# A new order of issue for a four-layer graph-attention kernel: the planner's durations read from a trace, and a weight-load term in every handoff to TensorE

## The chip, the cores and the metric

The kernel runs on one core of one Trainium2 chip. The metric is the time of one execution on the device in microseconds (us); less is better. The time of a version is the median of its runs.

## What is computed

The input `x` is 128 graphs of 64 nodes with 512 features in 32-bit floats, 8192 rows in all; `adj` is one 64x64 adjacency that all graphs share. Four layers follow one another, each of the same outer form:

```python
h = jnp.maximum(_layernorm(x, axis=-1), 0.0)
x = x + layer(h, adj, ...)
```

Layers 0 and 1 are attention with 8 heads of 64 features inside each graph, masked by `adj` (q, k, v projections of 512x512, softmax over 64 neighbours, weighted sum; layer 1 has an output projection too). Layer 2 has no softmax:

```python
rel = jnp.einsum('bnd,bmd->bnm', q, k)
rel = adjacency.T[None, :, :] * rel
rel = rel / jnp.linalg.norm(rel, axis=2, keepdims=True)
return jnp.einsum('bnm,bmd->bnd', rel, v)
```

Layer 3 is masked attention like layer 1 with an output projection `o`, and returns `o + layernorm(o)`.

## The kernel before

The rows are cut into 16 pieces of 512 rows (8 graphs each); 16 pieces by 4 layers make 64 turns of the main loop, `n` from 0 to 63. The activations pass from layer to layer through DRAM. In each turn a piece is normalised, transposed by a 16-bit DMA transposition (`turn`: a copy to `z` on VectorE or ScalarE, the transposition `hp<-z` on SyncE's queue, a copy back to `hT` or `s` on ScalarE), and projected. A projection is a fast matrix product: seven products of halves instead of eight, and three of the seven are cut once more (`prod_2`). For that GpSimd and VectorE form sums of inputs (`S` and `S2` from `hT`, `SO` and `SO2` from `oT`) and of weights, and ScalarE, VectorE and GpSimd recombine the products that lie in PSUM into `qT`, `kT`, `v`, `xo` and small helpers `p5`. A step that takes products out of a PSUM bank is called an eviction here (`kT<-mm`, `v<-mm` and so on). Scores (`mm<-kT,qT`) and weighted values (`mm<-s,v` or `mm<-v,s`) are blocks of small 64x64 products; `attend` between them is the softmax on all four engines.

No line of the kernel issues an instruction directly. `pe`, `dve`, `act`, `gps` and `plan.sync` are recorders: each call becomes a step of a `Plan` (`record`, `add`), with what it must wait for, a duration and a delay to its users, both from `duration`. A run of matmuls between `plan.begin()` and `plan.end()` is one step, a block. `Plan.order` then puts all 13,182 steps in an order: it walks through time, and takes for the engine that can start first the ready step that can start first, and among steps that can start equally early the one with the lowest `rank`. The rank is the latest time a step may have for the matmuls that need it, plus `PREFER`, a table with an offset in ns for some kinds of step, less `HASTE` for a step of another engine that reads PSUM. The same walk gives each block its PSUM bank out of eight; `WINDOW` limits how many banks out of turn may be opened. `issue` then issues in that order. Each engine runs its own instructions strictly in the order of issue and waits on semaphores where data or banks need it. So the table and the durations are guesses at build time: they decide the order and the banks, and nothing else. All instructions carry the line of `issue`, L285, in the profile, so groups are told apart by tiles.

The two numbers that a step leaves for its users are used like this:

```python
ready[u] = max(ready[u], at + busy - lag + (0.0 if same and not moves else late))
last[h] = max(last.get(h, 0.0), at + busy + (0.0 if e == "tensor" else late))
```

The first is the time at which the user `u` is taken to be ready, the second the time at which a PSUM bank is taken to be free again.

Of the kernel before, what the change touches and what calls it, by code (L numbers as in the profile page):

```python
# [21 lines left out]
D = 512  # L22
# [34 lines left out]
class Plan:  # L57
# [106 lines left out]
    def order(self):  # L164
# [58 lines left out]
        while len(self.start) < n:  # L223
# [40 lines left out]
            for h in uses[i]:  # L264
                last[h] = max(last.get(h, 0.0), at + busy + (0.0 if e == "tensor" else late))
                left[h] -= 1
                if not left[h]:
                    del holds[self.bank[h]]
                    freed[self.bank[h]] = last[h]
            for u, lag in users[i]:  # L270
                same = self.steps[u][0] == e
                ready[u] = max(ready[u], at + busy - lag + (0.0 if same and not moves else late))
                wait[u] -= 1
                if not wait[u]:
                    here[self.steps[u][0]].append(u)
# [35 lines left out]
class Pool:  # L311
# [28 lines left out]
PORT = 150.5  # L340
# [6 lines left out]
WINDOW = 6  # L347
RESERVE = 0
HASTE = 0.0
PREFER = {  # L350
    "gps dma_start out_0_dram<-xo 2048": -12683,
    "gps dma_start x1<-kT": -7145,
    "gps dma_start x1<-row": -3460,
    "gps dma_start x1<-xo": -18648,
    "gps memset mhalf<- 8": 4917,
    "gps memset ones<- 1": -3867,
    "gps tensor_scalar ve<-mv 1": 622,
    "gps tensor_scalar ve<-mv 4": -1287,
    "gps tensor_tensor S2<-S 128": 9247,
    "gps tensor_tensor S2<-S2 128": -37406,  # L360
    "gps tensor_tensor S<-S 512": -89087,
    "gps tensor_tensor S<-hT 512": -1496,
    "gps tensor_tensor SO2<-SO 128": 12636,
    "gps tensor_tensor SO2<-SO2 128": 10398,
    "gps tensor_tensor SO<-oT 512": 2203,
    "gps tensor_tensor hT<-hT 128": 1226,
    "gps tensor_tensor kT<-kT 128": 5636,
    "gps tensor_tensor kT<-kT 256": 3369,
    "gps tensor_tensor kT<-kT 512": -42897,
    "gps tensor_tensor oT<-oT 128": 2476,  # L370
    "gps tensor_tensor qT<-qT 128": -134,
    "gps tensor_tensor qT<-qT 256": -1241,
    "gps tensor_tensor rn<-ss 8": -17140,
    "gps tensor_tensor row<-hT 128": -1603,
    "gps tensor_tensor row<-row 128": 8443,
    "gps tensor_tensor rs<-ve 1": 12875,
    "gps tensor_tensor s<-hT 128": -26189,
    "gps tensor_tensor s<-s 1024": -13182,
    "gps tensor_tensor s<-s 128": -40765,
    "gps tensor_tensor v<-v 128": -615,  # L380
    "gps tensor_tensor w<-w 128": -892,
    "gps tensor_tensor w<-w 512": 3785,
    "gps tensor_tensor xo<-xo 128": 44131,
    "gps tensor_tensor xo<-xo 512": -445,
    "sca activation kT<-mm 128": -119261,
    "sca activation kT<-mm 256": -39612,
    "sca activation qT<-mm 128": -41982,
    "sca activation qT<-mm 256": -11513,
    "sca activation s<-s 1024": 49040,
    "sca activation s<-s 256": 11077,  # L390
    "sca activation xin<-xin 512": 38622,
    "sca copy hT<-hp 1024": 66109,
    "sca copy hT<-mm 512": 10088,
    "sca copy kT<-mm 128": -16208,
    "sca copy kT<-mm 512": -19133,
    "sca copy oT<-mm 512": -12905,
    "sca copy p5<-mm 128": 237,
    "sca copy qT<-mm 128": 625,
    "sca copy qT<-mm 256": 54924,
    "sca copy qT<-mm 512": 3166,  # L400
    "sca copy s<-hp 1024": 447,
    "sca copy s<-mm 512": 10472,
    "sca copy v<-mm 128": 7235,
    "sca copy v<-mm 256": -3409,
    "sca copy v<-mm 512": -11450,
    "sca copy w<-mm 128": -19703,
    "sca copy w<-mm 256": -8441,
    "sca copy xo<-mm 128": 3488,
    "sca copy xo<-mm 256": -4935,
    "sca copy z<-mm 512": 4852,  # L410
    "sca copy z<-s 1024": 11870,
    "syn dma_start SO<-in_L2_gnn_Wk_dram": -11583,
    "syn dma_start a2d<-z": 2446,
    "syn dma_start adj2<-in_adj_dram": 31047,
    "syn dma_start bk0<-in_L0_gnn_bk_dram": 17099,
    "syn dma_start bk1<-in_L1_gnn_bk_dram": 6479,
    "syn dma_start bq0<-in_L0_gnn_bq_dram": -9211,
    "syn dma_start bq1<-in_L1_gnn_bq_dram": 6149,
    "syn dma_start bv1<-in_L1_gnn_bv_dram": 5734,
    "syn dma_start hp<-z": -502,  # L420
    "syn dma_start oT<-in_L2_gnn_Wq_dram": 4334,
    "syn dma_start oT<-in_L2_gnn_Wv_dram": 17636,
    "syn dma_start out_0_dram<-qT": 14773,
    "syn dma_start out_0_dram<-xo": 16686,
    "syn dma_start row<-in_L0_gnn_bv_dram": -25453,
    "syn dma_start row<-in_L3_gnn_ln_beta_dram": -11958,
    "syn dma_start row<-in_L3_gnn_ln_gamma_dram": -3573,
    "syn dma_start w<-a2d": -3983,
    "syn dma_start w<-in_L0_gnn_Wk_dram": 15922,
    "syn dma_start w<-in_L0_gnn_Wq_dram": 27053,  # L430
    "syn dma_start w<-in_L0_gnn_Wv_dram": -942,
    "syn dma_start w<-in_L1_gnn_Wk_dram": -1089,
    "syn dma_start w<-in_L1_gnn_Wo_dram": 29403,
    "syn dma_start w<-in_L1_gnn_Wq_dram": 6765,
    "syn dma_start w<-in_L3_gnn_w_proj_dram": 1486,
    "syn dma_start w<-in_L3_gnn_w_qkv_dram": 11967,
    "syn dma_start xin<-in_x_dram": -293,
    "syn dma_start xin<-out_0_dram": -4629,
    "syn dma_start xin<-x1": -1001,
    "syn dma_start xo<-x1": 599,  # L440
    "ten matmul mm<-S 128": -809,
    "ten matmul mm<-S 256": 1010,
    "ten matmul mm<-SO 128": 6386,
    "ten matmul mm<-SO 256": -1770,
    "ten matmul mm<-hT 128": 131,
    "ten matmul mm<-hT 256": -309,
    "ten matmul mm<-hT 64": 100821,
    "ten matmul mm<-oT 128": 538,
    "ten matmul mm<-oT 256": -850,
    "ten matmul mm<-oT 512": -47270,  # L450
    "ten matmul mm<-qT 64": -5718,
    "ten matmul mm<-row 128": -1010,
    "ten matmul mm<-s 1": 29205,
    "ten matmul mm<-s 128": 916,
    "ten matmul mm<-s 64": 12446,
    "ten matmul mm<-v 64": 3123,
    "ten matmul mm<-w 128": 589,
    "ten matmul mm<-w 256": 3762,
    "ten transpose mm<- 128": 3312,
    "ten transpose mm<-s 128": 34074,  # L460
    "vec bn_aggr mv<-st 2": 22606,
    "vec bn_stats st<-kT 6": 32606,
    "vec bn_stats st<-w 6": 180,
    "vec bn_stats st<-xin 6": 18172,
    "vec reciprocal sr<-sr 16": -12420,
    "vec scalar_tensor_tensor nb<-mv 1": -6732,
    "vec scalar_tensor_tensor nb<-mv 4": 407,
    "vec scalar_tensor_tensor qT<-z 512": 11775,
    "vec scalar_tensor_tensor xo<-mm 256": -18855,
    "vec scalar_tensor_tensor xo<-z 512": 2344,  # L470
    "vec scalar_tensor_tensor z<-kT 512": -2532,
    "vec scalar_tensor_tensor z<-w 512": -7120,
    "vec tensor_copy hT<-mm 512": -34134,
    "vec tensor_copy ss<-mm 4": -8958,
    "vec tensor_copy z<-oT 1024": -28676,
    "vec tensor_copy z<-xin 1024": -1765,
    "vec tensor_reduce mx<-s 16": -1296,
    "vec tensor_reduce sr<-s 16": -539,
    "vec tensor_scalar mask0<-adj2 64": -460,
    "vec tensor_scalar mask1<-adj2 64": 7823,  # L480
    "vec tensor_scalar mask1<-mask1 64": -2796,
    "vec tensor_scalar mask3<-adj2 64": 3491,
    "vec tensor_tensor S2<-hT 128": -8365,
    "vec tensor_tensor S<-S 512": -9486,
    "vec tensor_tensor S<-hT 512": 846,
    "vec tensor_tensor SO2<-oT 128": 21917,
    "vec tensor_tensor hT<-hT 128": 12751,
    "vec tensor_tensor kT<-mm 128": -2068,
    "vec tensor_tensor kT<-mm 512": -895,
    "vec tensor_tensor oT<-mm 512": 569,  # L490
    "vec tensor_tensor oT<-oT 128": 19236,
    "vec tensor_tensor p5<-mm 128": -44354,
    "vec tensor_tensor qT<-mm 128": 1804,
    "vec tensor_tensor qT<-mm 256": 12827,
    "vec tensor_tensor qT<-mm 512": -35526,
    "vec tensor_tensor qT<-qT 512": 13240,
    "vec tensor_tensor s<-mm 512": 311,
    "vec tensor_tensor v<-mm 128": -36409,
    "vec tensor_tensor v<-mm 256": -7501,
    "vec tensor_tensor v<-mm 512": -84,  # L500
    "vec tensor_tensor w<-mm 128": -22071,
    "vec tensor_tensor w<-mm 256": 2131,
    "vec tensor_tensor w<-mm 512": -831,
    "vec tensor_tensor w<-w 128": -8652,
    "vec tensor_tensor w<-w 512": 30518,
# [9 lines left out]
def duration(eng, op, aps, a, k):  # L515
# [3 lines left out]
    if eng == "tensor":  # L519
        kdim, m = aps[1].partition_size(), aps[1].free_size()  # L520
        if op == "transpose":
            return 109, 200
# [1026 lines left out]
```

## Time and profile before

| what | value |
|---|---|
| runs before (three) | 2804.97, 2805.68, 2806.94 us; median 2805.68 |
| the profiled execution: its own time, its span | 2805.3 us, 2803.5 us |
| TensorE matmul busy | 2758.9 us, 98% of the span, 29,259 records |
| TensorE weight load busy (beside the matmuls) | 2506.2 us, 89% |
| VectorE, ScalarE, GpSimd busy | 2185.6 us (78%), 1691.6 us (60%), 1999.4 us (71%) |
| mean granted TensorE clock | 0.999 |
| DMA engines, mean busy share by slice | 0.4 to 0.7 |

The table's busy times are sums over instructions as the profile draws them. Matmul ends are modelled and overlap, so that busy share is no measure of how tightly the matmuls follow each other; starts are. `PE` is the matmul, `PEld` the load of its weights, `DVE` VectorE, `ACT` ScalarE, `POOL` GpSimd, `SP` SyncE with its DMA queue. A bracket behind a row gives the idle time before it and what ended it.

### The profile page before, as it was taken

The page shows a single profiled execution, that of the slowest core. Times are in us where ns is not written, and L with a number is a line of the kernel's source. Part 1 is how long each engine was busy: PE and PEld are TensorE (multiplying, and loading weights), DVE is VectorE, ACT ScalarE, POOL GpSimd, SP SyncE. Part 2 cuts the span into 40 slices and gives each one's busy share as a digit, 9 for nine tenths or more (in the row PEclk, how much of TensorE's full clock was granted, in tenths as well). Part 3 has the DMA queues.
Part 4 walks back from the last instruction along what each step waited for, and adds up shares of the span by engine and source line. Part 5 has one row for each costly group of instructions (what it writes and reads, how often), then busy time and mean ns, then how long its engine had stood idle before and what let it go on. Part 6 is the DMA issues. An engine that isn't in the chain of part 4 may idle for free. (4 is left out here: it accounts for less than half of the span.)

```text
span 2803.5 us, 72722 instructions
## 1 busy us (share of the span) xinstructions
PE 2758.9 (98%) x29259; PEld 2506.2 (89%) x29259; DVE 2185.6 (78%) x4436; ACT 1691.6 (60%) x2885; POOL 1999.4 (71%) x2381
## 2 busy tenths in 40 slices
PE   9999999999999999999999999999999999999998
PEld 8889888988898999999999898989899899898897
DVE  7877778877877777777777666666788998988998
ACT  5677677777665665666755454445555655565662
POOL 5667767668977767677679855556777887887885
PEclk9999999999999999999999999999999999999999
DMA  5765566666466455464566675656545655655655
GB/s 140 155 144 132 145 145 147 150 135 143 95 116 119 91 117 97 94 133 88 100 150 128 158 180 147 166 135 163 110 76 92 114 99 92 116 97 91 116 86 113
DMA packets 635026, 344.54 MB, mean 123 GB/s; under 512 B 484288, under 2 KB 565952, under 8 KB 634688
## 3 DMA queue, kind: packets, MB, share of 16 engines
q1 hardware_dynamic: 601424, 273.83, 42.8%
q0 software_dynamic: 33264, 66.06, 14.7%
q8 instruction: 230, 3.77, 0.5%
q14 instruction: 108, 0.88, 0.1%
HBM read 120.63 MB, written 102.76 MB: 80 GB/s over the span
## 5 line engine op out<-in xcount | busy, mean ns | idle before, releaser
L285 PE MATMUL mm<-S,w 128*128 128x256 f32 (+1 forms) x4600 | 907.0, 338 | 9.2 <-ACT kT L285 6.2
L285 PEld LDWEIGHTS mm<-S,w 128*128 128x128 f32 x4600 | 732.0, 191 | 74.7 <-ACT kT L285 9.6
L285 PE MATMUL mm<-hT,w 128*128 128x128 f32 (+1 forms) x3392 | 605.2, 310 | 5.9 <-ACT kT L285 2.0
L285 PEld LDWEIGHTS mm<-hT,w 128*128 128x128 f32 x3392 | 520.5, 191 | 51.7 <-ACT p L285 2.7
L285 PE MATMUL mm<-w,S 128*128 128x256 f32 (+1 forms) x2604 | 520.4, 339 | 0.8 <-ACT v L285 0.7
L285 PEld LDWEIGHTS mm<-w,S 128*128 128x128 f32 x2604 | 419.0, 191 | 37.5 <-issue 1.0
L285 DVE TENSOR_TENSOR qT<-mm,qT 128x128 f32<-128x128 f32 (+2 forms) x578 | 264.4, 485 | 173.4 <-PE mm L285 82.6
L285 PE MATMUL mm<-w,hT 128*128 128x128 f32 (+1 forms) x1872 | 343.1, 315 | 6.2 <-DVE v L285 4.4
L285 DVE TENSOR_TENSOR kT<-mm,kT 128x512 f32<-128x512 f32 (+2 forms) x616 | 274.4, 471 | 91.3 <-ACT kT L285 68.1
L285 ACT COPY v<-mm 128x128 f32<-128x128 f32 (+1 forms) x380 | 169.4, 447 | 291.7 <-PE mm L285 262.9
L285 ACT COPY hT<-hp 128x1024 uint16<-128x1024 uint16 x252 | 331.0, 1354 | 17.3 <-DMA hp<-z 15.1
L285 PEld LDWEIGHTS mm<-w,hT 128*128 128x128 f32 x1872 | 287.1, 191 | 31.0 <-issue 3.6
L285 DVE TENSOR_TENSOR v<-mm,v 128x512 f32<-128x512 f32 (+2 forms) x578 | 261.1, 480 | 61.9 <-PE mm L285 25.8
L285 PE MATMUL mm<-w,SO 128*128 128x256 f32 x1302 | 262.0, 336 | 5.2 <-DVE kT L285 5.0
L285 POOL TENSOR_TENSOR s<-s,mx 128x1024 f32<-128x1024 f32 x96 | 186.8, 1947 | 109.4 <-DVE mx L285 87.0
L285 ACT ACTIVATE xin<-xin,nb,rs 128x512 f32<-128x512 f32 x256 | 198.8, 814 | 98.5 <-DVE nb L285 98.5
L285 ACT COPY s<-hp 128x1024 uint16<-128x1024 uint16 x188 | 246.2, 1353 | 0.0
L285 POOL TENSOR_TENSOR qT<-qT,p 128x256 f32<-128x256 f32 (+1 forms) x170 | 110.0, 659 | 185.4 <-DVE qT L285 105.5
L285 PEld LDWEIGHTS mm<-w,SO 128*128 128x128 f32 x1302 | 213.6, 191 | 28.5 <-DVE kT L285 10.4
L285 DVE COPY z<-xin 128x1024 uint16<-128x1024 uint16 x252 | 197.8, 801 | 30.3 <-ACT xin L285 29.6
L285 ACT COPY z<-s 128x1024 uint16<-128x1024 uint16 x188 | 191.6, 1049 | 26.4 <-POOL s L285 26.2
L285 POOL TENSOR_TENSOR v<-v,p 128x256 f32<-128x256 f32 (+1 forms) x170 | 124.3, 742 | 96.4 <-DVE v L285 86.1
(120 smaller groups left out, 4685.9 us busy)
## 6 DMA issues: line engine op xcount, KB each, us to landing
xin<-x SPq DMA_DIRECT2D x128, 256.0 KB, 4.7
xin<-in_x_dram SPq DMA_DIRECT2D x64, 256.0 KB, 3.9
x<-row POOLq DMA_DIRECT2D x16, 1024.0 KB, 16.9
xin<-out_dram SPq DMA_DIRECT2D x64, 256.0 KB, 3.9
out_dram<-row POOLq DMA_DIRECT2D x16, 1024.0 KB, 9.3
x<-xo POOLq DMA_DIRECT2D x15, 1024.0 KB, 12.3
out_dram<-xo POOLq DMA_DIRECT2D x15, 1024.0 KB, 9.3
xo<-in_x_dram SPq DMA_DIRECT2D x32, 256.0 KB, 3.9
```

The costliest lines, as they stand in the source:

```text
L285: getattr(getattr(self.nc, eng), op)(*a, **k)
```

## The change

The steps, their instructions and what each must wait for stay as they are. What is changed is what the planner is told, and so the order of issue and the banks:

- A new constant, `LOAD = 110` ns, is added to the delay of every handoff from another engine to TensorE, and to the time at which another engine frees a PSUM bank.
- The durations and delays in `duration` are new, most by a few per cent. Delays of VectorE go from 150 to 160 ns, of ScalarE from 170 to 180 or 200, of GpSimd from 120 to 130; the `PORT` delay from 150.5 to 160.5.
- `WINDOW` goes from 6 to 7 and `HASTE` from 0 to 1865 ns.
- The whole table `PREFER` (some 160 entries) is new.
- The block in `relate` is planned 580 instead of 300 ns longer than its matmuls.

```diff
-                last[h] = max(last.get(h, 0.0), at + busy + (0.0 if e == "tensor" else late))
+                last[h] = max(last.get(h, 0.0), at + busy + (0.0 if e == "tensor" else late + LOAD))
...
                 same = self.steps[u][0] == e
-                ready[u] = max(ready[u], at + busy - lag + (0.0 if same and not moves else late))
+                load = LOAD if self.steps[u][0] == "tensor" else 0.0
+                ready[u] = max(ready[u], at + busy - lag + (0.0 if same and not moves else late + load))
...
-PORT = 150.5
+PORT = 160.5
+LOAD = 110
...
-WINDOW = 6
+WINDOW = 7
 RESERVE = 0
-HASTE = 0.0
+HASTE = 1865.0
 PREFER = {
...
-    "gps tensor_tensor S<-S 512": -89087,
+    "gps tensor_tensor S<-S 512": -646,
...
-    "sca activation xin<-xin 512": 38622,
+    "sca activation xin<-xin 512": 12304,
...
-    "vec tensor_tensor kT<-mm 512": -895,
+    "vec tensor_tensor kT<-mm 512": -1303,
...
-    fixed = {"scalar_tensor_tensor": 140, "tensor_reduce": 100}.get(op, 85)
+    fixed = {"scalar_tensor_tensor": 125, "tensor_reduce": 100}.get(op, 68)
...
-        return fixed + n * 1.01, PORT if two else 150
+        return fixed + n * 1.04, PORT if two else 160
...
-        return max(240 + 0.49 * n, (1.32 if out.dtype == U16 else 1.4 if own else 0.95) * n), 170
+        if out.dtype == U16:
+            return (947 if out.ap[-1][0] == 1 else 1211), 200
+        if psum:
+            return (55 + 0.836 * n, 180) if op == "copy" else (175 + 0.711 * n, 180)
+        return (717 if isinstance(k.get("scale"), bass.AP) else 105 + 0.834 * n), 180
...
-            return (1030 if ALU.pow in a else 250), 120
-        return 1.82 * n if n > D else 170 + 2.1 * n, 120
+            return (385 + 156.5 * n if ALU.pow in a else 200), 130
+        return 1.82 * n if n > D else 143 + 2.13 * n, 130
...
-        plan.end(300)
+        plan.end(580)
```

More of the change, by code (lines that the diff above doesn't have):

```diff
@@ L346 @@
 ON_DVE = "2"
-WINDOW = 6
+WINDOW = 7
 RESERVE = 0
-HASTE = 0.0
+HASTE = 1865.0
 PREFER = {
[L351 to L360, printed above, removed]
-    "gps tensor_tensor S<-S 512": -89087,
[L362 to L390, printed above, removed]
-    "sca activation xin<-xin 512": 38622,
[L392 to L488, printed above, removed]
-    "vec tensor_tensor kT<-mm 512": -895,
[L490 to L505, printed above, removed]
-    "vec tensor_tensor xo<-mm 128": -8130,
-    "vec tensor_tensor xo<-mm 512": 843,
@@ new lines @@
+    "gps dma_start out_0_dram<-row 2048": -5236,
+    "gps dma_start out_0_dram<-xo 2048": -402,
+    "gps dma_start x1<-kT": -8963,
+    "gps dma_start x1<-row": 1362,
+    "gps dma_start x1<-xo": -9912,
+    "gps tensor_scalar ve<-mv 1": -564,
+    "gps tensor_tensor S2<-S 128": 3948,
+    "gps tensor_tensor S2<-S2 128": -5548,
+    "gps tensor_tensor S<-S 128": 11385,
+    "gps tensor_tensor S<-S 512": -646,
+    "gps tensor_tensor S<-hT 512": 589,
+    "gps tensor_tensor SO2<-SO 128": -17575,
@@ new lines @@
+    "gps tensor_tensor SO2<-SO2 128": -2154,
+    "gps tensor_tensor SO<-SO 128": -411,
+    "gps tensor_tensor SO<-oT 512": -362,
+    "gps tensor_tensor hT<-hT 128": 3311,
+    "gps tensor_tensor kT<-kT 128": -98339,
+    "gps tensor_tensor kT<-kT 512": -2966,
+    "gps tensor_tensor qT<-qT 128": -5579,
+    "gps tensor_tensor qT<-qT 256": 9110,
+    "gps tensor_tensor rn<-ss 8": -34892,
+    "gps tensor_tensor row<-hT 128": 664,
+    "gps tensor_tensor row<-row 128": 928,
+    "gps tensor_tensor rs<-ve 1": 47293,
@@ new lines @@
+    "gps tensor_tensor rs<-ve 4": -1991,
+    "gps tensor_tensor s<-hT 128": 1720,
+    "gps tensor_tensor s<-s 1024": -27587,
+    "gps tensor_tensor s<-s 128": -447,
+    "gps tensor_tensor v<-v 128": -51403,
+    "gps tensor_tensor v<-v 256": 1536,
+    "gps tensor_tensor w<-w 128": -3400,
+    "gps tensor_tensor w<-w 256": -2153,
+    "gps tensor_tensor w<-w 512": -7294,
+    "gps tensor_tensor xo<-xo 128": -3829,
+    "gps tensor_tensor xo<-xo 256": -17821,
+    "gps tensor_tensor xo<-xo 512": -24461,
@@ new lines @@
+    "sca activation kT<-mm 128": 3117,
+    "sca activation kT<-mm 256": -44222,
+    "sca activation qT<-mm 128": -3862,
+    "sca activation qT<-mm 256": 7208,
+    "sca activation s<-s 1024": -9262,
+    "sca activation s<-s 256": 461,
+    "sca activation xin<-xin 512": 12304,
+    "sca copy hT<-hp 1024": 72415,
+    "sca copy hT<-mm 512": -23177,
+    "sca copy kT<-mm 128": 26150,
+    "sca copy kT<-mm 256": -8365,
+    "sca copy kT<-mm 512": 12936,
+    "sca copy oT<-mm 512": 24886,
+    "sca copy qT<-mm 256": -9312,
@@ new lines @@
+    "sca copy qT<-mm 512": 9418,
+    "sca copy s<-hp 1024": -12125,
+    "sca copy v<-mm 128": 1565,
+    "sca copy v<-mm 512": -4871,
+    "sca copy w<-mm 128": 23360,
+    "sca copy w<-mm 256": -22055,
+    "sca copy xo<-mm 128": -291,
+    "sca copy xo<-mm 256": -422,
+    "sca copy xo<-mm 512": -6652,
+    "sca copy z<-hp 1024": 2677,
+    "sca copy z<-mm 512": -2648,
+    "sca copy z<-s 1024": 1031,
+    "syn dma_start SO<-in_L2_gnn_Wk_dram": -5858,
+    "syn dma_start a2d<-z": 238,
+    "syn dma_start adj2<-in_adj_dram": 19924,
@@ new lines @@
+    "syn dma_start bk0<-in_L0_gnn_bk_dram": -7662,
+    "syn dma_start bk1<-in_L1_gnn_bk_dram": 24005,
+    "syn dma_start bq0<-in_L0_gnn_bq_dram": -9601,
+    "syn dma_start bq1<-in_L1_gnn_bq_dram": 2267,
+    "syn dma_start bv1<-in_L1_gnn_bv_dram": -5413,
+    "syn dma_start hp<-z": -14040,
+    "syn dma_start oT<-in_L2_gnn_Wq_dram": -137,
+    "syn dma_start oT<-in_L2_gnn_Wv_dram": 1006,
+    "syn dma_start out_0_dram<-qT": 14975,
+    "syn dma_start out_0_dram<-xo": -3753,
+    "syn dma_start qT<-out_0_dram": -1103,
@@ new lines @@
+    "syn dma_start row<-in_L0_gnn_bv_dram": -1956,
+    "syn dma_start row<-in_L1_gnn_bo_dram": 15474,
+    "syn dma_start row<-in_L3_gnn_b_proj_dram": 48446,
+    "syn dma_start row<-in_L3_gnn_ln_beta_dram": 996,
+    "syn dma_start row<-in_L3_gnn_ln_gamma_dram": -407,
+    "syn dma_start v2d<-z": -7041,
+    "syn dma_start w<-a2d": 1418,
+    "syn dma_start w<-in_L0_gnn_Wq_dram": -2601,
+    "syn dma_start w<-in_L1_gnn_Wo_dram": 1769,
+    "syn dma_start w<-in_L1_gnn_Wq_dram": 9073,
+    "syn dma_start w<-in_L1_gnn_Wv_dram": 11420,
@@ new lines @@
+    "syn dma_start w<-in_L3_gnn_w_proj_dram": -68065,
+    "syn dma_start w<-in_L3_gnn_w_qkv_dram": -15968,
+    "syn dma_start w<-v2d": 1945,
+    "syn dma_start x1<-xo": -1980,
+    "syn dma_start xin<-out_0_dram": 419,
+    "syn dma_start xin<-x1": 4125,
+    "syn dma_start xo<-in_x_dram": 3226,
+    "ten matmul mm<-S 128": -1756,
+    "ten matmul mm<-S 256": -2237,
+    "ten matmul mm<-SO 128": -25324,
+    "ten matmul mm<-SO 256": 3911,
+    "ten matmul mm<-hT 128": -1890,
+    "ten matmul mm<-hT 256": -4791,
@@ new lines @@
+    "ten matmul mm<-hT 64": 5281,
+    "ten matmul mm<-oT 128": 166,
+    "ten matmul mm<-oT 256": 902,
+    "ten matmul mm<-oT 512": -3738,
+    "ten matmul mm<-qT 64": -9650,
+    "ten matmul mm<-row 128": 814,
+    "ten matmul mm<-s 1": -772,
+    "ten matmul mm<-s 128": -1583,
+    "ten matmul mm<-s 64": -322,
+    "ten matmul mm<-v 64": -2194,
+    "ten matmul mm<-w 128": -2728,
+    "ten matmul mm<-w 256": 122,
+    "ten transpose mm<- 128": 3003,
+    "ten transpose mm<-s 128": 46899,
+    "vec bn_aggr mv<-st 2": 8545,
@@ new lines @@
+    "vec bn_stats st<-kT 6": -4460,
+    "vec bn_stats st<-w 6": 1794,
+    "vec bn_stats st<-xin 6": 3400,
+    "vec reciprocal sr<-sr 16": -1441,
+    "vec scalar_tensor_tensor nb<-mv 1": 2908,
+    "vec scalar_tensor_tensor nb<-mv 4": 28681,
+    "vec scalar_tensor_tensor qT<-z 512": 7083,
+    "vec scalar_tensor_tensor xo<-mm 256": -7371,
+    "vec scalar_tensor_tensor xo<-z 512": 7183,
+    "vec scalar_tensor_tensor z<-kT 512": 1942,
+    "vec scalar_tensor_tensor z<-w 512": -4197,
+    "vec tensor_copy hT<-mm 512": -12340,
@@ new lines @@
+    "vec tensor_copy ss<-mm 4": -17501,
+    "vec tensor_copy z<-oT 1024": -5577,
+    "vec tensor_copy z<-xin 1024": 1873,
+    "vec tensor_reduce mx<-s 16": -4675,
+    "vec tensor_reduce sr<-s 16": 4365,
+    "vec tensor_scalar mask0<-adj2 64": -27966,
+    "vec tensor_scalar mask1<-adj2 64": 30017,
+    "vec tensor_scalar mask1<-mask1 64": -2192,
+    "vec tensor_scalar mask3<-adj2 64": 4793,
+    "vec tensor_tensor S2<-hT 128": 1361,
+    "vec tensor_tensor S<-S 512": 16008,
+    "vec tensor_tensor S<-hT 512": -3270,
@@ new lines @@
+    "vec tensor_tensor SO2<-oT 128": -4614,
+    "vec tensor_tensor hT<-hT 128": 3837,
+    "vec tensor_tensor kT<-mm 256": 264,
+    "vec tensor_tensor kT<-mm 512": -1303,
+    "vec tensor_tensor oT<-mm 512": -3325,
+    "vec tensor_tensor p5<-mm 128": 1705,
+    "vec tensor_tensor qT<-mm 128": -9592,
+    "vec tensor_tensor qT<-mm 256": -67522,
+    "vec tensor_tensor qT<-mm 512": 968,
+    "vec tensor_tensor qT<-qT 512": -4383,
+    "vec tensor_tensor s<-mm 256": -13475,
+    "vec tensor_tensor s<-mm 512": -1670,
@@ L508 @@
+    "vec tensor_tensor v<-mm 128": 1205,
+    "vec tensor_tensor v<-mm 512": 9746,
+    "vec tensor_tensor w<-mm 128": -10221,
+    "vec tensor_tensor w<-mm 256": -8521,
+    "vec tensor_tensor w<-mm 512": -2557,
+    "vec tensor_tensor w<-w 128": 11030,
+    "vec tensor_tensor w<-w 512": -351,
+    "vec tensor_tensor xo<-mm 128": 3603,
+    "vec tensor_tensor xo<-mm 256": -6352,
 }
@@ L518, in duration @@
     n = out.free_size()
+    psum = any("PSUM" in str(v.space) for v in aps[1:])
     if eng == "tensor":
@@ L521, in duration @@
         if op == "transpose":
-            return 109, 200
-        pass_ = max(n * 0.842, 111 if m > HD else HD * 0.842)
+            return 109, 220
+        pass_ = max(n * 0.8438, 111.8 if m > HD else HD * 0.842)
         if m <= HD:
-            pass_ = pass_ / (2 if kdim > HD else 4) + 1
-        return 2 * pass_, 200
+            pass_ = pass_ / (2 if kdim > HD else 4) + 1.3
+        return 2 * pass_, 220
     if eng == "vector":
         n = max([n] + [v.free_size() for v in aps[1:]])
+        two = sum("PSUM" not in str(v.space) for v in aps[1:]) > 1
         if op == "bn_stats":
-            return 590, 150
+            return 595, 160
         if n <= HD:
-            return 120, 150
+            return (90 if op == "bn_aggr" else 170), PORT if two and op == "scalar_tensor_tensor" else 160
         if out.dtype == U16:
             return 0.67 * n, PORT
-        fixed = {"scalar_tensor_tensor": 140, "tensor_reduce": 100}.get(op, 85)
+        fixed = {"scalar_tensor_tensor": 125, "tensor_reduce": 100}.get(op, 68)
         two = sum("PSUM" not in str(v.space) and v.free_size() > HD for v in aps[1:]) > 1
-        return fixed + n * 1.01, PORT if two else 150
+        return fixed + n * 1.04, PORT if two else 160
     if eng == "scalar":
-        own = isinstance(k.get("scale"), bass.AP)
-        return max(240 + 0.49 * n, (1.32 if out.dtype == U16 else 1.4 if own else 0.95) * n), 170
+        if out.dtype == U16:
[3 more added lines that the diff above has]
+        return (717 if isinstance(k.get("scale"), bass.AP) else 105 + 0.834 * n), 180
     if eng == "gpsimd" and op != "dma_start":
         if n <= HD:
-            return (1030 if ALU.pow in a else 250), 120
-        return 1.82 * n if n > D else 170 + 2.1 * n, 120
+            return (385 + 156.5 * n if ALU.pow in a else 200), 130
+        return 1.82 * n if n > D else 143 + 2.13 * n, 130
     size = (2 if out.dtype == U16 else 4) * n * out.partition_size()
     if "accum_op" in k:
-        return 1100, 2000 + size / 150
+        return 950, 2000 + size / 150
     return 1270 if k.get("transpose") else 520, size
```

## The prediction

> **What bounds the kernel now.** I read the profile's head first.
>
> ```profile
> span 2803.5 us, 72722 instructions
> PE 2758.9 (98%) x29259; PEld 2506.2 (89%) x29259; DVE 2185.6 (78%) x4436; ACT 1691.6 (60%) x2885; POOL 1999.4 (71%) x2381
> PEclk9999999999999999999999999999999999999999
> ```
>
> TensorE is busy throughout, at full clock. Its order cannot shorten the matmuls, so the question is how much time lies between them. Busy shares don't tell that; starts do. In the trace a 256-column matmul is followed by the next start after 215 to 216 ns, a 128-column one after 111 to 112 ns. I took each pair of neighbours and summed what goes beyond the usual gap of its kind: 43.9 us between blocks, 40.5 us inside blocks, 84.4 us in all. The rest closes: first matmul at 1.4 us, 2708.7 us of gap-free work, 84.4 us, 8.6 us after the last matmul, sum 2803.1 of 2803.5.
>
> What can a new order touch of the 84.4? I looked for blocks that start over 40 ns late and begin right after a producer on another engine. There are 72: 38.0 us at the block's first matmul and 7.2 us directly behind it, 45.1 us. The start-up has 4.5. The other 35 lie inside blocks, mostly where no producer is late (15 of it in the 64-column blocks); I let them stand. The waits of the weight load name the producers (columns: us in total, times, longest):
>
> ```profile
> PEld mm L285 <- DVE kT L285: 17.4, 42, 0.9
> PEld mm L285 <- ACT kT L285: 12.2, 16, 2.2
> PEld mm L285 <- DVE v L285: 5.1, 7, 1.6
> PEld mm L285 <- ACT p L285: 4.3, 5, 1.2
> ```
>
> They are evictions of PSUM, above all of `kT`. The timeline shows why they are late. In layer 3 the same picture comes once per turn:
>
> ```profile
> 2395.25 3.07 DVE L285 TENSOR_TENSOR SO<-oT 128x128 f32<-128x128 f32 x1
> 2395.27 2.20 POOL L285 TENSOR_TENSOR s<-s,mx 128x1024 f32<-128x1024 f32 x1
> 2398.24 0.41 DVE L285 TENSOR_TENSOR v<-mm,v 128x256 f32<-128x256 f32 x1
> 2398.57 0.68 DVE L285 TENSOR_TENSOR kT<-mm,row 128x512 f32<-128x512 f32 x1
> 2399.30 1.56 PE L285 MATMUL mm<-w,SO 128*128 128x256 f32 x6 [0.38 <-DVE kT L285]
> ```
>
> A 128x128 addition that takes 0.28 us at its shortest takes 3.07 beside a large GpSimd instruction; two evictions queue behind it, and TensorE waits. In layer 0 it is ScalarE's order:
>
> ```profile
> 568.86 0.82 ACT L285 ACTIVATE xin<-xin,nb,rs 128x512 f32<-128x512 f32 x1
> 569.58 0.84 ACT L285 ACTIVATE kT<-mm,bk 128x256 f32<-128x256 f32 x2
> 570.46 0.30 PEld L285 LDWEIGHTS mm<-S,w 128*128 128x128 f32 x2 [2.05 <-ACT kT L285]
> ```
>
> A normalisation goes ahead of the two evictions that TensorE waits for.
>
> **Part by part.** No part adds or removes a step: 13,182 with the same dependencies, so TensorE's gap-free work stays at 2708.7 us, the bytes moved too. What moves is places: 1158 of 2310 TensorE blocks keep theirs, 809 of 4436 VectorE, 785 of 2884 ScalarE, 462 of 2375 GpSimd steps, and 713 of SyncE's 1177 DMAs.
>
> *The order.* For each block I counted the cover of its handoffs: the TensorE work that the program puts between the block that releases the producer and the block that needs it, less the producer's median duration in the trace, counted also from one and from two instructions ahead in the producer's queue, the least of the three. I did it for both orders, and put beside it the stall that the trace of before shows on the blocks of each class (blocks before, stall before, blocks after):
>
> - under 800 ns: 93, 28.3 us; 55
> - 800 to 1000: 113, 1.8 us; 138
> - 1000 to 1500: 282, 18.0 us; 207
> - 1500 to 2500: 387, 15.6 us; 410
> - above: 1400, 16.5 us; 1465
>
> With the mean stall of each class the new counts give 16.7 + 2.2 + 13.2 + 16.5 + 17.3 = 65.9 us, against 80.2: a gain of 14. The first class is mixed, though: of its pairs, `kT` on ScalarE into a block of `w` (14 pairs, 4.8 us) go to 4, `kT` with bias on ScalarE (10 pairs, 10.4 us) to none, `v` 128 wide into `hT` (3, 3.2 us) to none, while pairs that never stalled stay. Pricing each pair that remains at its own rate, and the 19 of a kind that before doesn't have in this class at the class mean of 0.30, the class costs 10.5 instead of 16.7: a gain of 20. The two families by name agree: the 14 `kT`-to-`SO` waits of layer 3 (8.8 us) go from a cover of 1.4 us (one 2.2) to 2.8 or more; of the 10 `kT`-copy waits (4.7 us) five go to 2.2 or more and five only from 0.8 to 1.1. Of all 72 late blocks 63 get more cover. Most of the thin ones that go are in the first 700 us (43 to 10).
>
> I take 18. The ends: if covers are followed through six queue places and three engines, the class under 400 ns grows from 32 to 38, and the same pricing gives a gain of only 5; if all 72 late blocks came on time and none were new, it would be 45. The value is nearer the short count because in the worst rows above the culprit stands one or two places ahead.
>
> *`LOAD`.* It is planning only and costs nothing itself. Is it real? In the trace 58 of 74 late starts come 51 to 55 ns after the producer's end and the next matmul is then about 104 ns late too; 12 come after 143 to 146 ns, with 75 more behind. So being late costs about 105 to 200 ns beyond the lateness. [...] Padding has a price where it makes the walk put a ready block aside, but another ready block then goes first and the sum of blocks doesn't change; I price it at nothing. With no other ready block it is 0.11 us a time, 8 us if it met as many blocks as are late now.
>
> *`HASTE`, `WINDOW`, the durations.* They act through the same counts. What `HASTE` pushes back is softmax, normalisation and input sums. Their chain ends in `copy s<-hp` and `copy hT<-hp`. In program order the TensorE work from the attention copy to its first user is at least 1.7 us before and 2.8 after (one in ten under 4.3, then 5.4); for `hT` at least 10.7 and 9.9 in all but one in twenty, with a least of 5.5 and then 2.8. Nothing is late in these by the count.
>
> *DMAs.* The least work between a transposition's issue and its copy falls from 3.5 to 2.0 us for `hT`, and rises from 3.0 to 3.3 for attention. ScalarE waits 15.1 us for transpositions now; were that doubled, it would be hidden by the covers just named, and cost up to 15 us where an eviction queues behind. I take nothing.
>
> *`relate` 580.* Sixteen blocks of layer 2, planned 280 ns longer each; between nothing and 16 x 0.28 = 4.5 us either way. I take nothing.
>
> **Sum.** Span 2803.5 - 18 = 2785.5; the execution has 1.8 us around its span (2805.3), so 2787.3; its median is 0.4 above: 2787.7, say 2788.
>
> **The rivals.** *The waits only change places.* The deep count's gain of 5 and a few unlucky DMAs leave 2800 to 2811. For it: the planner's durations shift by a few per cent only, and the table is fitted to them. Against: the families with names get 1.4 us more cover, far beyond such an error.
>
> *Slower: blocked additions in layer 3.* VectorE is busy 318.5 of 350 us from 2100 on. There are 100 small additions of two SBUF operands after 2100 us, 50 us over their shortest time. Now one per turn runs into an eviction. If the new order lays three more of the kind into evictions with under 3 us of cover, each costs 0.63 (8.8 over 14): 3 x 14 x 0.63 = 26 us, and the gain outside layer 3 (some 10) is overdrawn: 2805.7 + 26 - 10 = 2822. It decides from a blocked time of 3 us per turn on, since the covers are 2.8 to 3.5. Against it: those covers are twice what they were.
>
> *Nearly all waits go.* 2805.7 - 45 = 2761, if the longest chains shorten too. The deep count speaks against it.
>
> **How the numbers follow.** A difference under 0.2% (5.6 us) can't be told from none. My forecast, a gain of 6 to 37 us (2768 to 2800): 0.70. Nearly all waits go (under 2768): 0.08. Change places (2800 to 2811): 0.09. Slower, at about 2822: 0.13. Faster is 0.70 + 0.08 = 0.78, same 0.09, slower 0.13. The range 2768 to 2811 holds the first and third, 0.79.
>
> **What would show it.** Right: the same busy time and matmul starts as now, the waits of the weight load for `kT` on VectorE and ScalarE (29.6 us together) at under half, most of the gain before 700 us and in layer 3. Wrong: those halved but the span not shorter (a new producer in the list, `s`, `hT` or `S`), or more small additions over 1 us on VectorE than now in layer 3, or fewer late blocks but more time inside blocks.

## The result and the profile after

The new order is slower, by 1.1%. Four runs took 2834.01 to 2840.87 us, median 2836.36, against 2806.11 for the kernel before (four runs, 2804.97 to 2806.94); the ratio is 1.011 (95% interval 1.0092 to 1.0128). The forecast was 2788. The profiled execution took 2836.85 us with a span of 2835.1. The same lines of the profile's head as before:

```profile
span 2835.1 us, 72716 instructions
...
PE 2767.2 (98%) x29259; PEld 2513.3 (89%) x29259; DVE 2207.7 (78%) x4436; ACT 1684.7 (59%) x2885; POOL 1983.4 (70%) x2381
...
PEclk9999999999999999999999999999999999999999
```

Same work, 31.6 us more span, and again a row of nines that hides what happened: the mean granted clock went from 0.999 to 0.995. The waits of the weight load (us in total, times, longest) do not hide it:

```profile
PEld mm L286 <- issue: 72.4, 133, 3.9
PEld mm L286 <- DVE kT L286: 12.5, 20, 1.7
PEld mm L286 <- ACT p L286: 6.3, 8, 1.0
PEld mm L286 <- ACT v L286: 5.0, 10, 1.3
...
PEld mm L286 <- DVE v L286: 1.5, 5, 0.5
```

The waits for `kT` fell from 29.6 to 12.7 us, as forecast (ScalarE's are 0.2, too small for this list). But the first line, which the prediction did not show, grew from

```profile
PEld mm L285 <- issue: 39.3, 110, 1.6
```

"issue" means that TensorE waited for nothing that has a semaphore in the trace. Its single waits now reach 3.9 us. To see how much of the loss it carries I made the prediction's account again: starts of neighbouring matmuls beyond their usual gap, sorted by what ended the gap (us, before and after).

```
                                            before  after
waits ended by an instruction fetch            1.4   14.4
other gaps at a half-clock stretch             0.0   13.1
block late behind a producer (72, 88 blocks)  38.0   46.9
directly behind such a block                   7.1    8.1
other gaps inside blocks                      33.6   28.3
start-up                                       4.5    4.2
all                                           84.4  114.9
```

The rows add up to within 0.2 us of the sum. The 30.5 us more are nearly the whole difference of the spans (31.6). Two rows need a word. The first is a narrow count: before's two stops of 1.5 us in layer 3 cannot both be in its 1.4. If it takes, behind the start-up, every gap over 0.3 us that no producer explains and that ends 1.1 to 1.7 us behind the end of an instruction packet (see below), it is 6.4 us before and 19.4 after; the difference is the same 13. The second is wider than the clock's own price: inside the six half-clock stretches ahead of the last microseconds the starts lose 1.4 to 1.7 us each, 9.4 in all; the rest are other gaps beside them.

By place: the start of the same blocks, after minus before, is +4 us at 109 us, -8 at 918, +1 at 1998, -2 at 2127, and +31 at 2768. Up to layer 3 gains and losses cancel, and the whole loss comes in layer 3's turns. There the same picture comes every third turn. The timeline of after, at the block of weighted values (64x64 products):

```profile
2152.66 1.27 POOL L286 DMA_DIRECT2D out_dram<-row  x1
...
2155.17 1.97 PE L286 MATMUL mm<-s,v 64*64 64x64 f32 x119
...
2160.76 0.25 PEld L286 LDWEIGHTS mm<-s,v 64*64 64x64 f32 x9 [3.75 <-issue]
2160.76 0.38 PE L286 MATMUL mm<-s,v 64*64 64x64 f32 x9 [3.62 <-issue]
```

The block of 128 products stops after 119, with all its data there. And the queues of the DMA view from 2146 to 2164 us (packets, MB, share of the 16 engines' time; then issues, KB each, us to landing):

```profile
q0 software_dynamic: 1056, 2.10, 78.0%
q8 instruction: 2, 0.03, 0.8%
...
out_dram<-xo POOLq DMA_DIRECT2D x1, 1024.0 KB, 9.2
out_dram<-row POOLq DMA_DIRECT2D x1, 1024.0 KB, 10.0
```

The instruction queue brings TensorE's instructions in packets of 16 KB, about 1 us each: before's trace has 58,880 instructions of TensorE and 230 such packets, 256 instructions a packet. A block of 128 of these small products is 256 instructions and takes 1.9 us when nothing stops it, so it uses up a packet in that time. In the stopped block the packet begins at 2158.41 us, 3.24 us after the block's start, takes 0.98, and the matmul starts 1.37 us after it. Until then the 16 engines carry two transfers of 1 MB that GpSimd's queue had issued 10.0 and 2.5 us ahead of the block: layer 3's accumulating sums into the output. In before the one from `row` is issued 8.0 us ahead of the block in 13 turns and the one from `xo` 30 us; the packets then come in time or nearly (longest stop 1.5 us). Right behind the stop follows a stretch at half clock. The table by stretches (from 2155, from 2162; PE to POOL busy, then PEclk):

```profile
2155.00:2162.00 7.00, 3.38 (x139) 3.06 (x138) 4.86 (x13) 2.18 (x5) 2.27 (x3) 1.00 0.92 145
2162.00:2166.00 4.00, 4.00 (x19) 3.61 (x18) 3.36 (x6) 0.51 (x2) 3.34 (x4) 0.57 0.02 5
```

Such a stretch lasts 3.41 us in the trace's clock records. Four of five in layer 3 stand at the four stops; before has none ahead of its last microseconds.

### The profile page after: what moved, and what is told of

Same layout as the page of the kernel before. It is cut to its first block, busy times and chain, and to the rows that moved or that the text cites. A ratio compares the mean times of both kernels' runs of the same rounds, so it can differ in the third digit from the quotient of the medians.

```text
span 2835.1 us, 72716 instructions
## 1 busy us (share of the span) xinstructions
PE 2767.2 (98%) x29259; PEld 2513.3 (89%) x29259; DVE 2207.7 (78%) x4436; ACT 1684.7 (59%) x2885; POOL 1983.4 (70%) x2381
## 4 chain that ended last, share of the span: by engine, by line
PE 67%; DVE 15%; POOL 8%; issue 4%; ACT 3%; DMA 2%; SPq 0%; DVEq 0%; POOLq 0%; ACTq 0%
PE mm L286 67%; DVE kT L286 3%; POOL s L286 3%; DVE st L286 2%; POOL S L286 2%; DVE z L286 2%; DVE qT L286 1%; DVE s L286 1%; DMA hp<-z 1%; DVE mx L286 1%; DVE v L286 1%; POOL v L286 1%; DVE S L286 1%; DVE sr L286 1%; DVE oT L286 1%
## 5 line engine op out<-in xcount | busy, mean ns | idle before, releaser
L286 PE MATMUL mm<-hT,w 128*128 128x128 f32 (+1 forms) x3392 | 612.6, 312 | 19.7 <-DVE v L286 8.6
L286 PEld LDWEIGHTS mm<-hT,w 128*128 128x128 f32 x3392 | 526.4, 192 | 70.0 <-issue 21.8
L286 PE MATMUL mm<-w,S 128*128 128x256 f32 (+1 forms) x2604 | 529.7, 339 | 2.5 <-ACT v L286 2.3
L286 DVE TENSOR_TENSOR qT<-mm,qT 128x256 f32<-128x256 f32 (+2 forms) x578 | 263.6, 485 | 160.8 <-ACT qT L286 79.3
L286 ACT COPY hT<-hp 128x1024 uint16<-128x1024 uint16 x252 | 335.2, 1357 | 31.6 <-DMA hp<-z 31.1
L286 PE MATMUL mm<-w,SO 128*128 128x128 f32 (+1 forms) x1302 | 251.1, 336 | 0.0
L286 DVE COPY z<-xin 128x1024 uint16<-128x1024 uint16 x252 | 206.9, 835 | 42.6 <-ACT xin L286 39.7
L286 POOL TENSOR_TENSOR S<-hT 128x512 f32<-128x512 f32 x126 | 164.7, 1307 | 101.4 <-ACT hT L286 95.6
L286 POOL TENSOR_TENSOR qT<-qT,p 128x128 f32<-128x128 f32 (+1 forms) x170 | 113.3, 680 | 161.8 <-DVE qT L286 127.6
```

The source lines that it names most:

```text
L286: getattr(getattr(self.nc, eng), op)(*a, **k)
```

## The experiments

Steps are numbered in program order. Theory A: the loss is made by the place of the accumulating transfers ahead of TensorE's instruction fetches, not by the order of the computing instructions. Theory B: VectorE's and GpSimd's computing instructions lie worse.

**Leave the transfers out, in both orders.** The 31 accumulating transfers of layer 3 are dropped at issue, so part of the output is not computed.

```diff
         for i in self.order():
             eng, calls = self.steps[i][:2]
+            if i > 9300 and "accum_op" in calls[0][2]:
+                continue
```

> The order after the change with the 31 accumulating DMAs of layer 3 left out (that part of the output is not computed); all else in place. Theory A: no fetch waits in layer 3 over 1 us, no half-clock windows there: about 2836 - 27 = 2809 or a little less. Theory B: 2836 less at most 3.

> The order before the change with the same 31 accumulating DMAs left out (that part of the output is not computed), as the control of the run before. Theory A: only the 1.3 to 2.9 us of fetch waits that before has in layer 3 go: 2803 to 2806. Then the two orders without the DMAs differ by no more than about 6 us, against 30 with them. Theory B: 2806, and 30 between the two.

Measured: the new order 2789.99 us, the old 2793.76, against 2806.34 for the full kernel before (ratios 0.9943, 0.9928 to 0.9957, and 0.9954, 0.9937 to 0.9971). So the transfers cost the new order 2836.4 - 2790.0 = 46 us and the old one 12.6. Without them the new order is ahead by 3.8 us (2788.66 to 2791.24 against 2791.61 to 2794.73), and in layer 3 it has no stop for instructions and no half-clock stretch. The late blocks then sum to 29.3 us (77) and 30.4 (57): the handoffs are nearly even.

The two orders come as close as theory A said (6 us or less), but both are faster than it said, by 19 us and by 9 to 12. Dropping a transfer also takes its issue, some 1.3 us, out of GpSimd's queue, and the late blocks shrank with it, from 46.9 to 29.3 us in the new order and from 38.0 to 30.4 in the old one. These two runs alone thus do not separate the fetches from the handoffs. One thing more is in the old order's trace without transfers: TensorE still stops for 1.2 to 1.4 us in or just behind three values blocks of layer 3 (until 2267.7, 2422.5 and 2577.5 us) and goes on 1.2 to 1.6 us behind the end of an instruction packet; in the 4 us ahead the DMA engines carry nothing but that packet. So short stops for instructions need no transfer in the way; in layer 3 the long ones came only with one near.

**Move the transfers near, in the old order.** Nothing but the 13 transfers from `row` moves, behind some computing GpSimd steps (the list is shortened).

```diff
-        for i in self.order():
+        order = self.order()
+        for i, j in MOVE.items():
+            order.remove(i)
+            order.insert(order.index(j), i)
+        for i in order:
...
+MOVE = {9848: 9994, 10096: 10242, 10344: 10490, ...}
```

> The order before the change, with the 13 row additions of layer 3 moved from 9 us to 3 us ahead of the block of weighted values, nothing else. Theory A: fetches that now start just ahead of the block start behind the added packets; where a fetch falls into or just behind the block, TensorE waits up to 4 us, so 13 turns give 15 to 45 us: 2821 to 2851, with waits that have no releaser and half-clock windows in the trace. Theory B: 2806 within 3 us, since no computing instruction changes place.

Measured: 2829.17 us, ratio 1.0081 (1.0063 to 1.0099), 23 us more, with 16.8 us of waits ended by a fetch and four half-clock stretches. Theory A (2821 to 2851) holds for the old order too. One detail is new: all 13 transfers are issued 2.7 us ahead, yet only every third turn stops (blocks at 2108.7, 2271.3, 2435.7, 2600.0 us; 3.2 to 4.2 us from one matmul's start to the next), three times within the first six matmuls behind the block and once at its product 125; the others lose 0.7 us within the block. So the place of the fetch counts as well.

**Move them later, in the new order.** The same edit, `MOVE = {10096: 10241, 10840: 10985, 11584: 11729, 12328: 12473}`: the four transfers from `row` go behind the block.

> The order after the change, with one thing moved: the four accumulating DMAs of layer 3 that add a row to the output 3.5 us ahead of a block of weighted values (about 2152.7, 2318.1, 2483.7 and 2649.3 us) go to a later place in GpSimd's queue, 6 to 7 us behind the start of that block. Nothing else changes place. Theory A (the instruction fetch of TensorE waits behind the packets of the accumulating DMAs, and the 64-column blocks run the queue dry): the four waits of 3.4 to 3.7 us without a releaser go (14.4 us) and with them most of the half-clock windows that follow (13.1 us of slow matmuls): 2836 falls to about 2811, and to 2822 if the clock dips are there by themselves. Theory B (the loss comes from small VectorE additions that are blocked beside GpSimd, and from late evictions): 2836 within 3 us.

Measured: 2836.61 us, ratio 1.0112 (1.0093 to 1.013). The waits for instructions are gone, and the time stays. The timeline shows a wait in their place:

```profile
2161.29 5.42 DVE L290 SCALAR_TENSOR_TENSOR xo<-z,rs,kT 128x512 f32<-128x512 f32 x2
...
2166.79 0.59 ACT L290 COPY kT<-mm 128x512 f32<-128x512 f32 x1 [8.29 <-DVE xo L290]
...
2167.43 1.59 PEld L290 LDWEIGHTS mm<-S,w 128*128 128x128 f32 x8 [3.94 <-ACT kT L290]
```

The later issue holds GpSimd up, its operations bunch, VectorE's two instructions take 5.42 us beside them (one of this kind takes 0.75 at the median in the new order's trace), and TensorE waits as long for `kT` as it had for instructions. Layer 3 again has five half-clock stretches, two at these waits and three at others. The time is the one that theory B named; but the waits for instructions went as theory A said, and new waits took their place. The cure was confounded, and the run by itself decides nothing.

**Move them earlier, in the new order.** In the same four turns `xo` goes to 20 us and `row` to 8 us ahead of the block.

```diff
+MOVE = {10095: 10141, 10096: 10058, 10839: 10885, 10840: 10802, 11583: 11597, 11584: 11667, 12327: 12373, 12328: 12290}
```

> The new order, but in the four turns of layer 3 in which both accumulating transfers stand just ahead of a 64-column block of weighted values, both are moved EARLIER in GpSimd's queue: the 1 MB transfer from xo from 11 to about 21 us ahead of the block, the one from row from 3.5 to about 9 us, as far as the order of before has its own. Nothing else moves. Theory A (TensorE's instruction fetch stands behind these transfers' packets, and the restart after such a wait brings a half-clock window): the waits of TensorE for instructions fall from 14.4 to under 4 us, the four half-clock windows of layer 3 that follow them go, no other wait takes their place since VectorE's additions keep their places, and the time falls by 18 to 26 us, to 2810 to 2818. Rival B (the losses of layer 3 come from VectorE and GpSimd, whose additions lie differently, and the clock follows from something else): no gain, 2830 to 2838. Were theory A true and the four additions blocked as when the transfers were moved later: 2830 to 2838 too, but with the waits at additions of VectorE and none for instructions.

Measured: 2816.99 us, ratio 1.0051 (1.0037 to 1.0065), in theory A's range. Eight transfers moved give back 19 of the 30 us. The same block in this run:

```profile
2150.19 1.97 PE L290 MATMUL mm<-s,v 64*64 64x64 f32 x119
...
2152.85 0.38 PE L290 MATMUL mm<-s,v 64*64 64x64 f32 x9 [0.69 <-issue]
```

It breaks at the same product, for 0.69 instead of 3.62 us; its packet begins at 2150.56, 0.37 us after the block's start instead of 3.24, and the matmul starts 1.34 us after the packet's end, nearly as in the new order (1.37). One half-clock stretch is left in layer 3. By the wider count above, the waits for instructions fall from 19.4 to 4.6 us and the loss inside half-clock stretches from 9.4 to 1.7, while the late blocks do not shrink: the gain is not made at the handoffs.

**Move one more issue.** Of what is left, 9.3 us lie at four blocks that wait for `v<-mm 256`, evictions behind a blocked addition:

```profile
2233.69 1.36 POOL L290 DMA_DIRECT2D out_dram<-xo  x1
...
2236.13 3.59 DVE L290 TENSOR_TENSOR oT<-oT 128x128 f32<-128x128 f32 x1
...
2242.62 1.75 DVE L290 TENSOR_TENSOR v<-mm,v 128x256 f32<-128x256 f32 x3
...
2243.13 1.97 PE L290 MATMUL mm<-hT,w 128*128 128x256 f32 x8 [2.09 <-DVE v L290]
```

```diff
+MOVE = {..., 10591: 10605, 11335: 11349, 12079: 12093, 12823: 12837}
```

> As the run with the transfers moved earlier in four turns (2817.0 us), and one more transfer from xo in four other turns moved about 6 us later, behind GpSimd's S<-hT addition, into the 1.85 us in which GpSimd waits for VectorE: the issue of 1.36 us no longer stands ahead of a run of GpSimd operations. Theory D (what is left of the loss is VectorE's small addition oT<-oT 128x128, 3.59 us beside that run of operations, behind which the eviction v<-mm 256 comes 2.3 us late, four times, with a half-clock window after one): those waits fall from 9.3 to under 2 us and the time by 7 to 13 us, to 2804 to 2810. Rival (the addition is held as long by GpSimd's own operations, without the issue): 2814 to 2819.

Measured: 2819.87 us, ratio 1.0054 (1.0041 to 1.0066): no gain. The four waits are gone (9.3 to 0), and the blocks that wait for `kT<-mm 512` went from 1.0 to 9.8 us:

```profile
2240.99 1.36 POOL L290 DMA_DIRECT2D out_dram<-xo  x1
...
2248.62 2.16 DVE L290 TENSOR_TENSOR hT<-hT 128x128 f32<-128x128 f32 x1 [2.41 <-POOL S L290]
...
2252.16 0.94 PE L290 MATMUL mm<-w,SO 128*128 128x128 f32 x6 [2.15 <-DVE kT L290]
```

GpSimd's `S` comes later, VectorE waits for it 2.41 us and is then blocked (2.16 us for an addition of 128x128). Theory D named the right chain, since its wait went with the issue, but not a saving; the time is just above the rival's range (2814 to 2819), though not for the rival's reason. Of the two places tried in this stretch of GpSimd's queue neither is free for 1.36 us, and these waits are 9 to 10 of the 12 to 16 us that are left of the loss.

**The term by itself.** `LOAD` set to 0 in the new kernel with all its other tables, with and without the transfers; the term alone in the old one; and small steps of it.

```diff
-LOAD = 110
+LOAD = 0
```

> The new order's own planner, durations and preferences, with LOAD set to 0 (the change without its weight-load term; the preferences stay those that were found with the term). The order is made anew: blocks that have under 800 ns of cover ahead of them are 162 instead of 55, and the accumulating transfers stand 2.6 to 5.7 us of TensorE's time ahead of the values blocks instead of 9 to 11. By the forecast's price of cover (14 us for 38 blocks fewer) the handoffs alone cost 40 us, 2876; by the price that the two runs without accumulating transfers gave (3.8 us for 38 blocks) 11 us. Theory A adds a wait for instructions in most of the eleven turns: 2 to 4 us each with its half-clock window, 20 to 40 us. Together 2855 to 2890; a time of 2836 or less would speak against both.

> The order made with LOAD set to 0, and without the 31 accumulating transfers of layer 3 (that part of the output is left out), to be set against the new order without them (2790.0 us): the weight-load term's worth at the handoffs by itself. Blocks with under 800 ns of cover: 162 against 55. Forecast's price of cover: 40 us, 2830. Price by the two runs without the transfers: 11 us, 2801. If the term is worth nothing: 2790. Waits for instructions stay under 2 us by theory A, and there are no half-clock windows in layer 3 unless the handoffs' own waits bring them.

> The kernel before with LOAD = 110 alone, put in the two places of the change; durations, preferences and WINDOW stay before's, and the order is made anew from them. Blocks with under 800 ns of cover: 81 against 93 of before. By the forecast's price (14 us for 38 blocks) the handoffs gain 4 us. The transfers from row come to stand 3.9 and 5.6 us of TensorE's time ahead of the values blocks, turn about, where before has 7.4 and the run with the row transfers near (23 us slower) 5.0 in all thirteen turns: theory A says 12 to 25 us lost there by waits for instructions, so 2812 to 2828 together. Rival C (what counts is whether the preferences were found with the same term: with the other value they cost as much as the new order lost with LOAD 0, up to 70 us, by late producers and the half-clock windows after them): 2840 to 2880, with the waits at producers and not for instructions.

> The new order's planner with LOAD = 100 in place of 110, all else as changed: 10 ns less in each handoff. The order made from it keeps 1873 of the new order's 2310 TensorE places and 2797 of 4436 on VectorE; blocks with under 800 ns of cover are 65 instead of 55, and layer 3 keeps both transfers just ahead of every third values block. Theory T (the term's size is what counts): 10 ns of 110 are worth a tenth of the 72 us that LOAD 0 cost, so 2836 to 2845. Theory F (the preferences fit one order, and any other order, however near the numbers that made it, has its handoffs where nobody fitted them): 20 us or more slower than the new order, 2856 and above.

> The order of before made anew with LOAD = 5, a twenty-second of the change's term. It keeps 2223 of 2310 TensorE places and 3450 of 4436 on VectorE; in layer 3 the transfers from row stay 7.4 us of TensorE's time ahead of the values blocks; blocks with under 800 ns of cover are 109 instead of 93. Theory T (the term's size counts): 3 us of the 66 us that LOAD 110 alone cost, so 2804 to 2812. Theory F (the preferences fit one order): 2820 and above, with waits at producers and none for instructions.

Measured, with the ratio to before:

```
new tables, LOAD 0                   2876.42   1.0255 (1.0241 to 1.0269)
  the same without the transfers     2861.94   1.02   (1.0186 to 1.0214)
new tables, LOAD 100                 2836.06   1.0102 (1.0083 to 1.0122)
old tables, LOAD 110                 2870.17   1.0235 (1.0219 to 1.025)
old tables, LOAD 5                   2812.40   1.0024 (1.0013 to 1.0036)
```

Without the transfers, taking the term out of the new tables costs 2861.9 - 2790.0 = 72 us, more than any price named for it (0, 11 or 40); with them, putting it into the old tables costs 66. So the term shows no price of its own: preferences that were found with one value lose with the other. Rival C, stated for the term alone in the old tables, holds: its waits for instructions are 1.8 us, its waits for `kT` on VectorE 27 us (17.4 before) and for `qT` on VectorE and `kT` on ScalarE 21 us each. Theory A's 12 to 25 us did not come there, though the transfers are issued 4.4 and 7.6 us ahead: these blocks stopped for late producers, and none for a fetch. Nor did my price of cover hold: 107 more thin blocks cost 72 us, 38 fewer gained 3.8, and 12 fewer, with the term in the old tables, came with a loss of 66.

The small steps decide less. With `LOAD` 100 the time is the same by a coincidence of two parts: the gaps grow by 15 us ahead of 2070 us and shrink by 16 behind it, where the nearest transfers now stand 1.2 us ahead of the block, nearer than before, and stop nothing (longest gap 0.6). With `LOAD` 5 the time ended 7 us up, at theory T's upper bound (2812) and below theory F's; that profile shows 10 us of fetch waits, most at score blocks of the earlier layers. Neither theory is settled by them.

**A version from both orders.** Before's order to step 289, the new one to 4625, before's to 8877, the new one to 10051, before's for layer 3's turns. The kernel issues from a list written out in it.

```diff
-        for i in self.order():
...
+        self.bank = dict(enumerate(listed[1]))
+        for i in listed[0]:
```

> The two orders spliced: before's up to step 289, the new one to step 4625, before's to 8877, the new one to 10051, and before's to the end, so that layer 3's turns are before's, with the accumulating transfers 7.4 us of TensorE's time ahead of the values blocks. The banks of PSUM keep the numbers that the source order gave, but for 20 of 1304. Over the stretches taken from the new order its run gained about 13 and 3 us on before's. Theory A (the new order is better at handoffs, and what it loses it loses in layer 3's turns by where the transfers stand): 2788 to 2797. Rival B (gains and losses of the stretches do not hold when the neighbours change, since each depends on which buffers and transfers the stretch inherits): 2803 to 2815.

Measured: 2797.27 us, ratio 0.9973 (0.9963 to 0.9983), faster than both kernels, by 7 and 39 us, 0.3 us above theory A's range. The stretches keep about half of the 16 us that they had gained in their own order.

## Why the prediction was wrong

*Right.* No step was added, and busy times stayed to within about 1%. The waits for `kT` fell to under half. The named pairs of `kT` into `SO` in layer 3 went (8.9 us to 0.5). The account by gaps carried over: the loss is the gaps' growth to within 1.1 us.

*The step that failed: "DMAs. I take nothing."* It weighed only SyncE's transpositions. GpSimd's queue also carries 31 accumulating transfers of 1 MB in layer 3, and what they would stand in the way of was not asked. Counting places in each engine's own order could not show it: the 16 transfers from `row` all keep their number in GpSimd's order, 13 of the 15 from `xo` move by 1 to 11 places, and yet in four turns the one from `row` is issued 2.5 to 2.9 us ahead of the values block instead of 8.0. The trace of before held the sign, at a values block of layer 3:

```profile
2581.28 2.29 PE L285 MATMUL mm<-s,v 64*64 64x64 f32 x125
...
2584.83 0.33 PE L285 MATMUL mm<-s,v 64*64 64x64 f32 x3 [1.26 <-issue]
```

Such stops were part of the 35 us that I "let stand". They stood because no producer is late there, and I took that for a cost that no order can touch. It depends on the order after all. Its price in the new order: 13 us more of fetch waits and some 6 of the 9.4 inside half-clock stretches, for the four that stand at the stops; the run with eight transfers moved earlier returns 19 us of the two together.

*The term that was mis-sized: the handoffs, 18 us.* Without the transfers it is 3.8; with them the late blocks did not shrink but grew, by 8.9 us. The gain was to come before 700 us and in layer 3; at 700 the new order is ahead by 1 or 2 us, at 918 by 8, and by 1998 that is gone. The handoffs named there went; but the count saw only order and median durations. New late blocks came where VectorE is blocked beside a run of GpSimd operations, for 3.6 us instead of 0.3: blocks that wait for `v<-mm 256` 9.2 us, for ScalarE's copy `qT<-mm 128` that is held up by VectorE 6.6 us, all in layer 3, none of either in before or without the transfers. The low end, a gain of 5 by the deep count, comes near the 3.8, but only with the transfers left out, and no run tests whether that is more than luck.

*The slower rival* named layer 3 and VectorE's blocked additions; they give about half of the loss there. But it expected more of them, and there are about as many: 13 of the additions of 128x128 take over 1 us after 2090 us, 12 before. They stand at other places. It missed what bunches GpSimd's operations, the 1.36 us of a transfer's issue (the run that moved one more issue shows this for the four waits for `v`), and its own price left out the clock.

*What would show it wrong* held: fewer waits by name, but more time inside blocks: what the 16 values blocks of layer 3 take beyond 1.88 us each went from 7.9 to 19.0 us.

## What to carry to other kernels

A reordering moves the issue of DMAs too, and a transfer's place can cost more than any handoff (in the new order four stops of 3.6 to 4.0 us from one matmul's start to the next, against 2.9 at most behind a late producer): list the big transfers and ask which engine's instruction fetch falls into each, above all ahead of blocks of many small matmuls (here 256 instructions, one packet, in 1.9 us). Read the idle time that no producer explains before letting it stand; a row "issue" of 3.75 us in the middle of a block was a late fetch here. To test a place, move the transfer both ways: one way may just trade the wait for another of the same length (here 3.94 us for `kT` in place of 3.75), and tables that were fitted together are only to be judged together.

## What the runs showed of the hardware

*Instruction fetch and GpSimd's transfers.* In the new order the 16 KB packet with TensorE's next instructions began 3.24 us behind the start of a values block, while the 1 MB accumulating transfers took 91% of the 16 engines' time (2152 to 2158.4 us); with the two transfers moved earlier it began 0.37 us behind. With the transfer from `row` issued 2.5 to 5.3 us ahead of a values block of layer 3, TensorE stopped in the block or just behind it for 2.4 to 4.2 us, from one start to the next, where its fetch fell there; in the other turns of the run that moved them near, 0.7 us were lost within the block; with the transfer 7.3 us or more ahead, or 1.2, the longest such stop was 1.7, and in the runs without the transfers 1.4.

*The clock.* In the 14 traces of all versions shown here there are half-clock stretches at 21 of 28 waits of TensorE over 2.9 us (from one matmul's start to the next), at 27 of 47 from 2.35 to 2.9 us, and at none under 2.24 us that has no longer wait beside it. Ahead of the last microseconds they last 3.41 us or a multiple. In the new order's trace six such stretches last 3.413 us each, and the starts lose 1.4 to 1.7 us inside each. Waits of 2.4 us, and twice 2.25, were enough here, so a wait of this length can cost up to another 1.7 us, half of a stretch.

*The blocked addition.* The row of 3.59 us above, for an addition that takes 0.27 at its shortest in the new order's trace, is longer than any one GpSimd instruction beside it (2.35 us the longest): it spans the end of one and three more behind it and ends 0.15 us after the last, so the addition seems to have waited through all four.
